# Local attention on Trainium2: the keys' copy on VectorE and the queries' copy between the exponentials, in the steps without an output projection

## Chip, core and metric

The kernel runs on one core of a Trainium2 chip. The metric is the device time of one execution in microseconds (us). Five engines with queues of their own work in parallel: TensorE (PE in the profile; its weight loads are PEld), VectorE (DVE), ScalarE (ACT), GpSimd (POOL) and SyncE (SP, which issues the DMAs).

## What is computed

The input is x with 8 batches of 512 rows and 256 columns, all in float32. Four residual blocks follow each other:

```
x = x + attention_a(layernorm(x))
x = x + layers(layernorm(x))
x = x + attention_b(layernorm(x))
x = x + layers(layernorm(x))
```

`layers` applies two layers, each a local attention and a feedforward part. The change lies in the local attention:

```
h = shift_token(x)
q, k, v = split(h @ wqkv)            # 8 heads of 64
q = l2norm(q) * qs ; k = l2norm(k) * ks
q, k = rotary_xpos(q, k)
# windows of 128 rows; a row sees its own window and the one before,
# masked to i - 128 <= j <= i
o = softmax(q k^T * 8, masked) v
x = x + o @ wo
```

The feedforward part is a layer norm, a product, a gate with GELU and a second product, added to x.

## The kernel before

**Stages.** The batches are worked in two groups of four. For each group the stages are: full attention (`attention_a`); then twice local attention (`attention_f`) and feedforward; then the second full attention (`attention_b`); then again twice local attention and feedforward. So there are eight stages of local attention. The profile names their tiles f0x, f0y, f1x and f1y (group, and first or second block); both layers of a block share a name.

**Tiles and steps.** A stage of local attention has 4 batches with 4 tiles of 128 rows each, 16 tiles in all (`nt`). One step of the loop in `run`, written out in `a_step`, works on three tiles at a time. For tile `step` it makes scores, softmax and values; this comes in two units of four heads each, `even` and `odd`. For tile `step + 1` it turns the rotated queries and keys so that the head dimension lies on the partitions (`turn_tile`, then `keep_tile`). For tile `step + 2` it makes the projections to queries, keys and values, the rotation and the norms. Steps -5 to -1 are handed out one by one to the stage before, which runs them among its own last steps. Steps 0 to 16 are the stage's own.

**One unit.** PE makes the scores (`scores`, L616). VectorE adds the mask and takes the maxima (`maxima`, four times L638), then L649 multiplies them by the inverse norm, with both inputs in SBUF. ScalarE makes four exponentials (`exponentials`, recorded at L241 of the helper `function`). In `divided`, VectorE takes the reciprocal of the sums (L719) and ScalarE divides (L735). PE turns the probabilities (`turn`, L681), VectorE copies them from PSUM (`keep_turned`, L692), and PE multiplies them with the values (`values`, L706).

**Around it.** `queries_and_keys` is the product at L510 (tile pqk). VectorE rotates it (`rotate`, L538 and L541), POOL adds both parts (`rotated`, twice L552), ScalarE squares (`squared`, L562), VectorE sums the squares (`norms`, L569), and POOL makes the inverse root (L266 and L267, of the helper `inv_sqrt`). The next step multiplies the keys by it on VectorE (`normalize_keys`, L583). `turn_tile` (L592) makes eight 128x128 turns into one PSUM tile of two banks, queries in one and keys in the other; `keep_tile` copies them to SBUF, both on ScalarE (L601 and L602). The scores of the next step read both copies. `keep_values` (L740), `project` (L748) and `add` (L755) are the output projection of a tile that is done.

**Order.** In steps 0 to 16 every instruction is chained to the one issued before it on its engine (`kept_order`), so each engine's queue is the order of the calls in `a_step`. The feedforward stage that follows lends pieces to steps 5 and 11 to 14 (`ahead()`), which are chained in the same way: in step 11 row statistics (L276 and L277), in step 12 the normalized rows hn (eight times L283), in step 13 one turn and its copy (L295 and L911). What the following stage issues after that is not chained on POOL. One such instruction is L923, which adds a bias to the rows y on POOL, 128x1024 elements, and which the builder has placed behind the inverse root of step 12. In the first layer, step 0 also normalizes the rows of a later batch (four times L283). POOL's adds at L552 wait by hand for the newest L649 (the list `marks`).

**Which steps project.** `project_next` makes one output projection a step. Steps 12 and 13 defer theirs to the last steps (`deferring`), and in step 0 none is due yet. Steps 14 to 16 have no new tile to project (`projecting` is false) and another order.

## Time and profile before

| what | us |
|---|---|
| median of 3 runs | 4423.52 (4421.06 to 4423.76) |
| the profiled execution | 4422.09 |
| its span in the trace | 4420.3 |
| busy: PE, DVE, ACT, POOL | 4195.3, 3100.1, 2699.3, 1175.5 |
| granted TensorE clock, mean | 0.993 of full speed |

The profile is one execution. A line of the timeline gives start, duration, engine, line of the code, operation, output and inputs, and how many neighbours were merged (x8). A bracket at its end tells how long the engine had stood idle before it and what ended that. [...] A line such as L241 can be that of a helper.

| line, engine | what | shape | us each |
|---|---|---|---|
| L601, ACT | copy of the turned queries | 128x512 from PSUM | 0.56 |
| L602, ACT | copy of the turned keys | 128x512 from PSUM | 0.58 |
| L740, DVE | copy of the values' product | 128x512 from PSUM | 0.68 |
| L569, DVE | sums of squares | 128x16 from 128x1024 | 1.21 |
| L267, POOL | power of -0.5 | 128x16 | 2.93 |
| L241, ACT | one exponential | 128x256 | 0.59 |

### The profile page before, as it was taken

To read this page: it belongs to the slowest core of one execution; us is meant where nothing else is said; L and a number is where in the kernel's file an instruction comes from. 1 tells how busy PE (TensorE), PEld (TensorE's weight loads), DVE (VectorE), ACT (ScalarE), POOL (GpSimd) and SP (SyncE) were. 2 spreads that over 40 slices of the span, in tenths; PEclk is the share of its full clock that TensorE was granted. 3 is DMA by queue.
4 is the path that set the end of the run, shared out by engine and by line. 5 is a ranking of instruction groups with operands and counts; after the bars stand their busy time and mean duration, and the time that the engine had idled before them with its cause. 6 is when DMAs were issued, how large, how long until landed. Compare 5 with 4: busy or idle time off the path is not lost.

```text
span 4420.3 us, 70595 instructions
## 1 busy us (share of the span) xinstructions
PE 4195.3 (95%) x26580; PEld 2536.5 (57%) x26580; DVE 3100.1 (70%) x7497; ACT 2699.3 (61%) x6316; POOL 1175.5 (27%) x1220
## 2 busy tenths in 40 slices
PE   9999999999888899999999999999999888999999
PEld 5666556655555465566566665565545554655655
DVE  6678737747999786377466786377479997863773
ACT  6777517716898675176167675276178996742761
POOL 0014214312222342143200242243122223422431
PEclk9999999999999999999999999999999999999999
DMA  2000000000000000000100000000000000000000
GB/s 82 1 22 4 23 3 23 3 24 20 2 1 1 20 4 7 4 22 13 53 30 1 20 3 24 22 4 23 5 21 1 2 1 20 4 6 23 3 4 23
DMA packets 51092, 63.36 MB, mean 14 GB/s; under 512 B 6336, under 2 KB 45504, under 8 KB 50752
## 3 DMA queue, kind: packets, MB, share of 16 engines
q1 hardware_dynamic: 50752, 58.85, 4.1%
q8 instruction: 211, 3.46, 0.3%
q14 instruction: 129, 1.06, 0.1%
HBM read 46.28 MB, written 4.19 MB: 11 GB/s over the span
## 4 chain that ended last, share of the span: by engine, by line
PE 74%; DVE 14%; ACT 9%; issue 1%; POOL 1%; DMA 0%; SPq 0%; POOLq 0%; ACTq 0%; DVEq 0%
PE pu_g1x L932 3%; PE pu_g0x L932 3%; PE pu_g0y L932 3%; PE pu_g1y L932 3%; PE s_a L389 3%; PE o_a L425 3%; PE ppt_a L414 3%; PE pqk_f1x L510 2%; PE pqk_f1y L510 2%; PE pqk_f0y L510 2%; PE pqk_f0x L510 2%; DVE pt_b L1274 2%; PE ppt_b L1269 2%; DVE r_b L1220 2%; PE pu_b L1085 1%; DVE num_b L1239 1%
## 5 line engine op out<-in xcount | busy, mean ns | idle before, releaser
L1269 PE MATMUL ppt_b<-ident,num_b 128*128 128x128 f32 x1280 | 227.5, 294 | 93.1 <-DVE pt_b L1274 63.3
L1269 PEld LDWEIGHTS ppt_b<-ident,num_b 128*128 128x128 f32 x1280 | 139.7, 144 | 279.3 <-ACT num_b L241 92.6
L241 ACT ACTIVATE num_b<-num_b,most_b 128x512 f32<-128x512 f32 (+3 forms) x512 | 280.6, 553 | 21.4 <-POOL most_b L1249 21.2
L1232 POOL TENSOR_TENSOR num_b<-num_b,causal 128x256 f32<-128x256 f32 x256 | 200.8, 797 | 258.9 <-ACT num_b L1226 258.9
L1274 DVE COPY pt_b<-ppt_b 128x512 f32<-128x512 f32 (+1 forms) x352 | 224.4, 637 | 36.8 <-PE ppt_b L1269 35.3
L1239 DVE CUSTOM_DVE_ANT_0 num_b<-num_b,r_b 128x512 f32<-128x512 f32 (+3 forms) x512 | 238.1, 512 | 3.7 <-POOL num_b L1232 3.7
L241 ACT ACTIVATE p_a<-s_a,nm_a 128x512 f32<-128x512 f32 x256 | 173.7, 683 | 105.0 <-DVE nm_a L393 101.9
L1216 DVE TENSOR_TENSOR t_b<-den_b,r_b 128x1024 f32<-128x1024 f32 (+1 forms) x176 | 197.3, 1121 | 25.9 <-ACT r_b L241 25.6
L1197 PE MATMUL den_b<-st_b,st_b 18*128 18x384 f32 (+3 forms) x1024 | 207.0, 476 | 7.5 <-ACT yT_b L1075 4.1
L1220 DVE SCALAR_TENSOR_TENSOR r_b<-t_b,r_b 128x1024 f32<-128x1024 f32 (+1 forms) x176 | 208.6, 1185 | 0.2
L393 DVE TENSOR_REDUCE nm_a<-s_a 128x2 f32<-128x1024 f32 x128 | 156.4, 1223 | 70.4 <-PE s_a L389 70.4
L241 ACT ACTIVATE r_b<-den_b 128x1024 f32<-128x1024 f32 (+1 forms) x176 | 165.8, 942 | 52.5 <-PE den_b L1197 30.1
L241 ACT ACTIVATE p_f0y<-p_f0y,nm_f0y,rn_f0y 128x256 f32<-128x256 f32 (+1 forms) x256 | 143.8, 563 | 80.6 <-DVE nm_f0y L649 80.5
L241 ACT ACTIVATE p_f1y<-p_f1y,nm_f1y,rn_f1y 128x256 f32<-128x256 f32 (+1 forms) x256 | 143.8, 563 | 80.6 <-DVE nm_f1y L649 80.5
L1197 PE MATMUL dot_b<-st_b,st_b 16*128 16x384 f32 (+3 forms) x1024 | 191.6, 475 | 0.0
L241 ACT ACTIVATE p_f1x<-p_f1x,nm_f1x,rn_f1x 128x256 f32<-128x256 f32 (+1 forms) x256 | 143.8, 564 | 76.0 <-DVE nm_f1x L649 75.9
L241 ACT ACTIVATE p_f0x<-p_f0x,nm_f0x,rn_f0x 128x256 f32<-128x256 f32 (+1 forms) x256 | 143.8, 564 | 75.3 <-DVE nm_f0x L649 75.2
L407 ACT ACTIVATE p_a<-p_a,sums_a 128x512 f32<-128x512 f32 x256 | 171.9, 719 | 26.5 <-DVE sums_a L405 26.5
L552 POOL TENSOR_TENSOR ro_f1x<-ro_f1x,rs_f1x 128x512 f32<-128x512 f32 x64 | 80.2, 1276 | 360.8 <-DVE rs_f1x L541 144.8
L552 POOL TENSOR_TENSOR ro_f0x<-ro_f0x,rs_f0x 128x512 f32<-128x512 f32 x64 | 80.2, 1275 | 360.6 <-DVE rs_f0x L541 144.8
L241 ACT ACTIVATE r_b<-r_b 128x1024 f32<-128x1024 f32 (+1 forms) x176 | 172.5, 980 | 5.7
L1226 ACT ACTIVATE num_b<-dot_b 128x1024 f32<-128x1024 f32 (+1 forms) x176 | 164.8, 937 | 3.1 <-PE dot_b L1197 3.1
(356 smaller groups left out, 11238.9 us busy)
## 6 DMA issues: line engine op xcount, KB each, us to landing
x<-in_x SPq DMA_DIRECT2D x8, 512.0 KB
out<-x SPq DMA_DIRECT2D x8, 512.0 KB
wf_0x<-in_f_wqkv SPq DMA_DIRECT2D x2, 1536.0 KB
wf_0y<-in_f_wqkv SPq DMA_DIRECT2D x2, 1536.0 KB
wf_1x<-in_f_wqkv SPq DMA_DIRECT2D x2, 1536.0 KB
wf_1y<-in_f_wqkv SPq DMA_DIRECT2D x2, 1536.0 KB
wg_0x<-in_f_w SPq DMA_DIRECT2D x2, 1386.0 KB
wg_0y<-in_f_w SPq DMA_DIRECT2D x2, 1386.0 KB
```

Of the source, the lines that this page charges most:

```text
L241: i = nc.scalar.activation(out, in_, func, **more).ins
L407: nc.scalar.activation(p[:, odd], p[:, odd], AF.Identity, scale=some[:, odd : odd + 1])
L510: nc.tensor.matmul(dst.rearrange("p h d -> p (h d)"), lhsT=hTs[b][:, k, t * P : (t + 1) * P], rhs=wqkv[:, k, c * INNER : (c + 1) * INNER], ...
L932: nc.tensor.matmul(pu[: cols.stop - cols.start, c], lhsT=w1[:, k, cols], rhs=hT[:, k, :], start=(k == 0), stop=(k == 1),)
L1197: return nc.tensor.matmul(s[:, a, m * width : (m + 1) * width], lhsT=left[at, j, past:width], rhs=right[at, j, :width], start=True, stop=True,
L1216: nc.vector.tensor_mul(t[:, :, :cols], den[:, :, :cols], r[:, :, :cols])
L1220: nc.vector.scalar_tensor_tensor(r[:, :, :cols], t[:, :, :cols], 2.0, r[:, :, :cols], ALU.subtract, ALU.mult)
L1226: nc.scalar.activation(num[:, :, :cols], dot[:, :, :cols], AF.Square, scale=-0.5)
L1232: nc.gpsimd.tensor_add(own, own, causal.unsqueeze(1).to_broadcast([P, 2, P]))
L1239: nc.vector.tensor_tensor_reduce(out=s4[:, a, m, :], in0=s4[:, a, m, :], in1=r4[:, a, m, :], scale=-1.0, scalar=LOWEST, op0=ALU.mult, op1= ...
L1269: nc.tensor.transpose(ppt[:, k, :], p[:, a, k * P : (k + 1) * P], ident)
L1274: nc.vector.tensor_copy(pt[:, a, :nblocks, :], ppt[:, :nblocks, :])
```

## The change

In steps 0, 12 and 13 of each stage (`light`) the order of the calls after the values' projection becomes: two of the four exponentials of the odd unit; `keep_values`; the turn of the even unit and its copy; the turn of the next tile; the queries' copy on ScalarE and the keys' copy on VectorE; the other two exponentials; the norms. Before, the order was: four exponentials, `keep_values`, the turn of the even unit and its copy, the norms, the turn of the next tile, and both copies on ScalarE. What comes after (`divided`, `values` and so on) is as it was. The other steps keep their order, and the work done is the same.

```diff
-        def keep_tile(at):
+        def keep_tile(at, by_vector=False):
...
             nc.scalar.copy(qT, pqt[:, 0])
-            nc.scalar.copy(kTs[b][:, :, t * P : (t + 1) * P], pqt[:, 1])
+            copy = nc.vector.tensor_copy if by_vector else nc.scalar.copy
+            copy(kTs[b][:, :, t * P : (t + 1) * P], pqt[:, 1])
...
-        def exponentials(unit):
+        def exponentials(unit, halves=(0, 1)):
...
-            p, nm, rn = ps[unit], nms.pop(unit), rns[at]
+            p, nm, rn = ps[unit], nms[unit], rns[at]
...
-            for odd in range(2):
+            for odd in halves:
...
             deferring = step in (nt - 4, nt - 3)
+
+            light = step == 0 or deferring
...
-            if projecting:
+            if projecting and light:
+                exponentials(odd, (0,))
+                on(keep_values, step - 1)
+                on(turn, even, nu)
+                on(keep_turned, even, nu)
+                on(turn_tile, step + 1)
+                keep_tile(step + 1, True)
+                exponentials(odd, (1,))
+                on(norms, step + 2)
+            elif projecting:
                 on(exponentials, odd, nu)
                 on(keep_values, step - 1)
                 on(turn, even, nu)
...
                     on(turn_tile, step + 1)
                     on(keep_tile, step + 1)
+            if projecting:
                 if not deferring:
                     project_next()
```

## The prediction

> **What bounds the kernel now.** I read the page's busy shares and its chain of work first, then the list of waits, then the timeline of one local-attention stage, of which the program has eight (two layers in each of four blocks).

> ```profile
> PE 4195.3 (95%) x26580; PEld 2536.5 (57%) x26580; DVE 3100.1 (70%) x7497; ACT 2699.3 (61%) x6316; POOL 1175.5 (27%) x1220
> PE 74%; DVE 14%; ACT 9%; issue 1%; POOL 1%; DMA 0%; SPq 0%; POOLq 0%; ACTq 0%; DVEq 0%
> ```

> TensorE (PE) carries three quarters of the chain; VectorE (DVE) and ScalarE (ACT) carry it only where PE stands idle. The change touches steps 0, 12 and 13 of each stage, 24 steps in all. Sixteen of them end in a PE wait for the keys' copy, eight of 1.59 us after step 0 and eight of 1.59 to 1.65 after step 12: 25.8 us, 0.58% of the span. That is the largest prize. The first stage:

> ```profile
> 316.16 0.57 ACT L601 COPY qT_f0x<-pqt_f0x 128x512 f32<-128x512 f32 x1
> 316.47 0.44 POOL L266 TENSOR_SCALAR rn_f0x<-ss_f0x 128x16 f32<-128x16 f32 x1
> 316.63 0.59 ACT L602 COPY kT_f0x<-pqt_f0x 128x512 f32<-128x512 f32 x1
> 317.11 1.29 ACT L735 ACTIVATE p_f0x<-p_f0x,sums_f0x 128x128 f32<-128x128 f32 x4
> 317.27 1.13 PE L616 MATMUL s_f0x<-kT_f0x,qT_f0x 64*128 64x256 f32 x8 [1.59 <-ACT kT_f0x L602]
> 318.33 0.66 PE L681 MATMUL ppt_f0x<-ident,p_f0x 128*128 128x128 f32 x4
> 318.83 3.60 PE L510 MATMUL pqk_f0x<-wf_0x,hT_f0x 128*128 128x512 f32 x8
> ...
> 479.11 0.69 DVE L692 COPY pt_f0x<-ppt_f0x 128x512 f32<-128x512 f32 x1
> 479.72 1.21 DVE L569 TENSOR_REDUCE ss_f0x<-sq_f0x 128x16 f32<-128x1024 f32 x1
> 481.21 0.18 DVE L719 RECIPROCAL sums_f0x<-sums_f0x 128x4 f32<-128x4 f32 x1 [0.28 <-ACT p_f0x L241]
> 481.27 0.27 POOL L266 TENSOR_SCALAR rn_f0x<-ss_f0x 128x16 f32<-128x16 f32 x1
> 481.63 3.03 POOL L267 TENSOR_TENSOR rn_f0x<-rn_f0x,neg_half 128x16 f32<-128x16 f32 x1
> 484.63 2.34 POOL L923 TENSOR_TENSOR y_0x<-y_0x,b 128x1024 f32<-128x1024 f32 x1
> 484.86 2.12 DVE L649 SCALAR_TENSOR_TENSOR nm_f0x<-nm_f0x,rn_f0x 128x4 f32<-128x4 f32 x1
> 486.91 0.68 DVE L583 TENSOR_TENSOR ro_f0x<-ro_f0x,rn_f0x 128x512 f32<-128x512 f32 x1
> 488.24 0.66 PE L706 MATMUL o_f0x<-pt_f0x,v_f0x 128*64 128x128 f32 x8 [0.91 <-DVE pt_f0x L692]
> ...
> 496.39 0.17 DVE L719 RECIPROCAL sums_f0x<-sums_f0x 128x4 f32<-128x4 f32 x1
> 496.47 0.57 ACT L602 COPY kT_f0x<-pqt_f0x 128x512 f32<-128x512 f32 x1
> 496.95 1.71 ACT L735 ACTIVATE p_f0x<-p_f0x,sums_f0x 128x256 f32<-128x256 f32 x4
> 497.51 1.64 PE L681 MATMUL ppt_f0x<-ident,p_f0x 128*128 128x128 f32 x8 [0.43 <-ACT p_f0x L735]
> ```

> Columns: start and duration in us, engine, line. Three things are to be seen. In step 0 the turns of the probabilities (L681) follow the scores closely, and they need the divisions (L735), which end at 318.40. After step 12 a 128x4 operation on VectorE takes 2.12 us: it stands until GpSimd's (POOL's) L923 ends at 486.97. Elsewhere the same line takes 0.16 to 0.17; all eight that start inside an L923 take 1.92 to 2.15. In step 13 VectorE's reciprocal (L719) follows the reduction L569 without a gap.

> **The parts and their prices.** ScalarE loses a copy that holds it 0.47 us (316.16 to 316.63 for its twin). VectorE gains one of 128x512 from PSUM: 0.68 to 0.69 in L692 and L740, with the next instruction 0.61 after its start. Both copies now stand ahead of the last two exponentials and wait for PE's turn of the tile; behind the one on VectorE are queued L569, the reciprocal and all later VectorE work; behind L569, POOL's two steps of the inverse root (L266, L267). No DMA is issued or moved, and SP's queue is not passed. The scores now wait for two engines; a semaphore instruction of PE's queue at L616 takes 0.05 us, so 0 to 0.05, hidden because the turns behind the scores wait for ACT anyway.

> Step 0. The tile's turn ends on PE at 315.08. Queries: 315.21 to 315.78. Keys: about 315.12 to 315.80. The scores can start at 315.85, 1.42 earlier, and end at 316.98. But L569 slides from 314.31 to 315.73, ends 316.94, and the reciprocal comes at 316.86 instead of 316.30. The divisions start 0.21 to 0.25 after a reciprocal where nothing else holds them (489.56 and 489.77), so at 317.1, where they were: what ACT gains by the lost copy, the late reciprocal takes. The fourth turn follows the fourth division at about 318.44, and the next projection (pqk) starts 0.13 later, at 318.57 instead of 318.83: **0.26 us won**. From there PE is nearly gapless to step 12, so the gain stays. POOL's root ends about 0.4 later (320.3), L583 waits until then; the copy behind it ends at 321.65, before PE wants it at 322.1: hidden.

> Step 12. Tile turned at 479.95 (478.91 and 1.04); keys on VectorE from 479.99, L569 at 480.60, ending at E = 481.81 instead of 480.93. L266 had been held by POOL's own add L552 to 481.18; now it follows E by 0.09 (so it does at 496.47, 496.56): 481.90, which is 0.63 later, and L267 and L923 with it. L923 starts 0.09 + 0.36 + 2.89 (the undisturbed stage) = 3.34 after E. The reciprocal starts 0.08 before E and L649 always 3.65 behind it (481.21 to 484.86; 837.56 to 841.21): E + 3.57. So L649 again finds L923 running and stands until it ends, 0.63 later than now; L583, the copy of the turned probabilities and PE's values (a wait of 0.91 now) go with it. The earlier scores are thus worth nothing here: **0.63 us lost** in seven stages. In the second stage L569 moves from 835.95 to 837.00 and L266 from 837.51 to 838.30: 0.79.

> Step 13. The tile's turn ends at 494.37, VectorE is free at 495.26; keys 495.26, L569 495.87 to 497.08, reciprocal 497.00, divisions 497.23 instead of 496.95. The turns and scores behind them, and the whole tail of the stage, wait on this: **0.28 us lost**. ACT's 0.47 was free to be won, but the late reciprocal takes it and more.

> Sum: 7 x (0.63 + 0.28 - 0.26) + (0.79 + 0.28 - 0.26) = 5.4 us. The profiled execution took 4422.09 (span 4420.3 and 1.8 around it), which makes 4427.5; the median of the runs shown, 4423.5, lies 1.4 higher, so 4428.9 against it, plus 0.12%. A measurement of this kernel can tell about 0.2%, 8.8 us, from no change; this is inside.

> [...]

> **Rivals.** (1) L649 gets in ahead of L923. L266 took 0.44 instead of 0.27 where it started 0.08 behind a VectorE row operation (316.47 above), as it now would in step 12, and L267 took 3.03 instead of 2.92 once: L923's lead of 0.23 could become -0.05. Then L649 takes 0.16 and the exponentials start 1.4 sooner; L583 still stands behind L923 (to about 487.75), the copy ends at 489.0, the reciprocal of step 13 comes 0.66 sooner, the keys' copy of step 13 takes 0.34 of that back, and the divisions start at 496.63: 0.32 won over both steps. With step 0, 0.58 a stage: -4.6 us, 4418.9. For it: the lead is within the scatter; against: POOL leads in most combinations, and L1220 is held up (1.71 instead of 1.22) where it starts 0.10 after a GpSimd operation.

> (2) Slower by over 0.2%: VectorE's copy is itself held by the rope add L552, beside which it runs in all three steps. Held to L552's end it would start 1.29, 1.2 and 1.03 us later (316.39, 481.18, 496.27), and some 1.2 + 1.84 + 1.31 us a stage would be lost: 35 us, 4458. It decides from 0.15 us held per copy (1.10 a stage). Against it: L692's copies that start beside L552 take 0.69 and 1.23, those that don't 0.68 and 1.22.

> (3) The wait goes, and PE keeps it: 25.8 us, 4398. Against it stand the divisions in step 0 and L923 in step 12.

> (4) Nothing: the edits cancel, within 2 us.

> **How the numbers follow.** Forecast 0.48, rival 1 0.30, rival 2 0.08, rival 3 0.08, rival 4 0.06. Bounds of the forecast: copy's hold 0.61 to 0.69, L266's delay 0 to 0.17, each passed on in steps 12 and 13: 0.5 to 1.0 a stage, 4427 to 4432. Rival 1 reaches down to 4416. The range 4416 to 4432 leaves out rivals 2 and 3, 0.16. Faster by over 0.2% is rival 3, 0.08; slower, rival 2, 0.08; within, the rest, 0.84.

> **What would show it.** Right: the 1.6 us waits of the scores gone after steps 0 and 12, pqk only 0.26 sooner; L569 1.4, 0.9 and 0.6 later; L923 0.6 later with L649 still about 2 us; divisions of step 13 0.28 later. Wrong: L649 of 0.16 after step 12 (rival 1); a keys' copy on VectorE over 0.8 us (rival 2); L923 elsewhere in POOL's queue, since it is not in the hand-written order and the build places it anew.

## The result and the profile after

| | before | changed |
|---|---|---|
| median, us | 4422.04 (5 runs, 4421.06 to 4423.76) | 4440.52 (5 runs, 4436.02 to 4442.29) |
| ratio | | 1.004 (95% interval 1.0029 to 1.005) |
| profiled execution: span, granted TensorE clock | 4420.3, 0.993 | 4438.7, 0.991 |

The changed kernel is 0.4% slower: 18.5 us where the forecast had 5.4, and above the range given (4416 to 4432). In the changed kernel the keys' copy is L603, and the lines behind it have moved: scores L617, maxima L639, L649 is now L650, the turns L682, their copy L693, values L707, reciprocal L720, divisions L736, and the bias add L923 is L936. The page's busy row and its chain:

```profile
PE 4212.5 (95%) x26580; PEld 2540.6 (57%) x26580; DVE 3116.4 (70%) x7521; ACT 2691.5 (61%) x6292; POOL 1177.7 (27%) x1220
PE 75%; DVE 14%; ACT 8%; issue 1%; POOL 1%; DMA 0%; SPq 0%; POOLq 0%; ACTq 0%; DVEq 0%
```

VectorE has 24 instructions more and ScalarE 24 fewer, as the change says. But PE, with the same 26580 matmuls, is busy for 17.2 us longer (4195.3 before). About half of this is no slower work: after steps 0 and 12 the four turns L682 now follow the divisions one by one, and their row counts 1.21 where it was 0.66 (some 9 us in all). The other half is in the products pqk and pv (together 9 us), which have become slower in places; no step of the prediction allowed for that.

Step 0 of the first stage, from the timeline of the changed kernel (start, duration, engine, line; the bracket is the idle time before it and what ended it; rows of one engine can overlap: L569 starts at 317.71, 0.08 before the 0.69 of L603 are over). The trace of the changed kernel runs 1.28 us behind that of before already at the start of this step, so a time of before is to be raised by 1.28 for a comparison.

```profile
316.49 0.58 ACT L601 COPY qT_f0x<-pqt_f0x 128x512 f32<-128x512 f32 x1
317.10 0.69 DVE L603 COPY kT_f0x<-pqt_f0x 128x512 f32<-128x512 f32 x1 [1.42 <-ACT qT_f0x L601]
317.71 1.21 DVE L569 TENSOR_REDUCE ss_f0x<-sq_f0x 128x16 f32<-128x1024 f32 x1
317.85 1.13 PE L617 MATMUL s_f0x<-kT_f0x,qT_f0x 64*128 64x256 f32 x8 [0.89 <-DVE kT_f0x L603]
318.83 0.17 DVE L720 RECIPROCAL sums_f0x<-sums_f0x 128x4 f32<-128x4 f32 x1
319.04 1.28 ACT L736 ACTIVATE p_f0x<-p_f0x,sums_f0x 128x128 f32<-128x128 f32 x4 [1.01 <-DVE sums_f0x L720]
319.49 1.21 PE L682 MATMUL ppt_f0x<-ident,p_f0x 128*128 128x128 f32 x4 [0.51 <-ACT p_f0x L736]
320.54 3.60 PE L510 MATMUL pqk_f0x<-wf_0x,hT_f0x 128*128 128x512 f32 x8
```

To be seen: the keys' copy on VectorE does not start with PE's turn, which ended at 316.37, but 0.03 after the end of the queries' copy on ScalarE. VectorE stands idle for 1.42 us ahead of it, and the sums of squares (L569) and the reciprocal (L720) stand behind it. The projection pqk comes 0.43 later than before (318.83 + 1.28 = 320.11), not 0.26 sooner.

Steps 12 and 13 of the same stage:

```profile
481.66 0.57 ACT L601 COPY qT_f0x<-pqt_f0x 128x512 f32<-128x512 f32 x1
482.26 0.69 DVE L603 COPY kT_f0x<-pqt_f0x 128x512 f32<-128x512 f32 x1 [0.92 <-ACT qT_f0x L601]
482.87 1.21 DVE L569 TENSOR_REDUCE ss_f0x<-sq_f0x 128x16 f32<-128x1024 f32 x1
...
484.00 0.17 DVE L720 RECIPROCAL sums_f0x<-sums_f0x 128x4 f32<-128x4 f32 x1
...
484.24 0.29 POOL L266 TENSOR_SCALAR rn_f0x<-ss_f0x 128x16 f32<-128x16 f32 x1 [1.50 <-DVE sums_f0x L720]
...
484.62 3.08 POOL L267 TENSOR_TENSOR rn_f0x<-rn_f0x,neg_half 128x16 f32<-128x16 f32 x1
...
487.60 0.16 DVE L650 SCALAR_TENSOR_TENSOR nm_f0x<-nm_f0x,rn_f0x 128x4 f32<-128x4 f32 x1
487.67 2.35 POOL L936 TENSOR_TENSOR y_0x<-y_0x,b 128x1024 f32<-128x1024 f32 x1
487.73 2.83 DVE L583 TENSOR_TENSOR ro_f0x<-ro_f0x,rn_f0x 128x512 f32<-128x512 f32 x1
...
490.49 0.68 DVE L693 COPY pt_f0x<-ppt_f0x 128x512 f32<-128x512 f32 x1
...
491.22 0.66 PE L707 MATMUL o_f0x<-pt_f0x,v_f0x 128*64 128x128 f32 x8 [1.92 <-DVE pt_f0x L693]
...
497.25 0.69 DVE L603 COPY kT_f0x<-pqt_f0x 128x512 f32<-128x512 f32 x1 [0.27 <-ACT qT_f0x L601]
```

The same wait stands in step 12 (idle 0.92) and step 13 (0.27). In 23 of the 24 steps the bracket of L603 names the queries' copy. And the meeting with the bias add went the other way: L650 gets in 0.07 ahead of L936 and takes 0.16, and L583, the next operation of VectorE, stands in its place until L936 ends (2.83 instead of 0.68). PE then waits 1.92 for the copied turns behind L583.

The third thing shows in the windows view of the changed kernel (columns: the stretch, its length, then busy us and count of PE, PEld, DVE, ACT and POOL, then the granted TensorE clock PEclk, DMA share and GB/s):

```profile
673.59:677.00 3.41, 2.01 (x19) 1.24 (x17) 2.50 (x6) 2.40 (x9) 1.96 (x4) 1.00 0.02 5
677.44:680.85 3.41, 3.41 (x7) 1.74 (x7) 1.68 (x7) 2.70 (x9) 2.30 (x1) 0.50 0.00 0
4271.24:4274.65 3.41, 1.50 (x14) 0.81 (x14) 3.41 (x4) 2.44 (x9) 1.34 (x2) 1.00 0.07 19
4275.09:4278.50 3.41, 3.41 (x8) 1.40 (x5) 3.03 (x12) 1.35 (x2) 0.80 (x1) 0.50 0.07 21
```

In the second and fourth row PE works for the whole 3.41 us, at half clock. The same product pqk that takes 3.60 elsewhere takes 5.02 there:

```profile
675.22 1.13 PE L617 MATMUL s_f0x<-kT_f0x,qT_f0x 64*128 64x256 f32 x8 [0.89 <-DVE kT_f0x L603]
676.87 1.36 PE L682 MATMUL ppt_f0x<-ident,p_f0x 128*128 128x128 f32 x4 [0.51 <-ACT p_f0x L736]
678.02 5.02 PE L510 MATMUL pqk_f0x<-wf_0x,hT_f0x 128*128 128x512 f32 x8
```

The profile of before has no such half-clock stretch in its eight stages of local attention; this one has seven. The next table splits the 18.4 us between the two spans: by how much PE's start of the same instruction moved against the profile of before, for each stage, from the product pv of step 0 to the first product of the feedforward.

| stage | step 0 | steps 12 and 13 | whole stage | what stands out |
|---|---|---|---|---|
| 1 | +0.43 | +0.69 | +0.98 | |
| 2 | +1.95 | +2.32 | +4.29 | half clock from 677.4 and 851.5; L650 stands for 2.26 |
| 3 | +0.43 | +1.74 | +2.42 | L650 stands for 2.26 |
| 4 | +2.13 | +0.68 | +2.80 | half clock from 1896.0 |
| 5 | +0.43 | +0.69 | +1.11 | half clock from 2691.3; PE's wait behind it shrinks to 0.37 |
| 6 | +0.43 | +0.68 | +1.10 | |
| 7 | +0.42 | +2.27 | +2.71 | half clock from 3913.3 |
| 8 | +1.99 | +2.34 | +4.34 | half clock from 4101.0 and 4275.1 |

Stages 1, 5 and 6 lose 1.0 to 1.1 us with nothing else to see in the time, which makes some 8.5 in eight. The two in which L650 stands lose about 1.1 more each, 2.2. What is left of the 19.75, some 9 us, falls on the half-clock stretches (1.5 to 1.7 us for one in step 0: 1.95, 2.13 and 1.99 against 0.43). The rest of the span adds 1.3 ahead of the first stage and takes 2.6 back between the stages.

### The profile page after: what moved, and what is told of

It reads as the page before. It is cut to its first block, busy times and chain, and to the rows that moved or that the text cites. A ratio compares the mean times of both kernels' runs of the same rounds, so it can differ in the third digit from the quotient of the medians.

```text
span 4438.7 us, 70599 instructions
## 1 busy us (share of the span) xinstructions
PE 4212.5 (95%) x26580; PEld 2540.6 (57%) x26580; DVE 3116.4 (70%) x7521; ACT 2691.5 (61%) x6292; POOL 1177.7 (27%) x1220
## 3 DMA queue, kind: packets, MB, share of 16 engines
q14 instruction: 129, 1.06, 0.1%
## 4 chain that ended last, share of the span: by engine, by line
PE 75%; DVE 14%; ACT 8%; issue 1%; POOL 1%; DMA 0%; SPq 0%; POOLq 0%; ACTq 0%; DVEq 0%
PE pu_g0x L945 3%; PE pu_g1x L945 3%; PE pu_g0y L945 3%; PE pu_g1y L945 3%; PE s_a L389 3%; PE o_a L425 3%; PE ppt_a L414 3%; PE pqk_f0x L510 2%; PE pqk_f1x L510 2%; PE pqk_f0y L510 2%; PE pqk_f1y L510 2%; PE ppt_b L1282 2%; DVE pt_b L1287 2%; DVE r_b L1233 2%; PE pu_b L1098 1%; DVE num_b L1252 1%
## 5 line engine op out<-in xcount | busy, mean ns | idle before, releaser
L241 ACT ACTIVATE num_b<-num_b,most_b 128x512 f32<-128x512 f32 (+3 forms) x512 | 280.6, 554 | 19.8 <-POOL most_b L1262 19.6
L241 ACT ACTIVATE p_a<-s_a,nm_a 128x512 f32<-128x512 f32 x256 | 173.7, 683 | 105.4 <-DVE nm_a L393 102.3
L241 ACT ACTIVATE r_b<-den_b 128x1024 f32<-128x1024 f32 (+1 forms) x176 | 165.8, 942 | 53.9 <-PE den_b L1210 31.4
L241 ACT ACTIVATE p_f0y<-p_f0y,nm_f0y,rn_f0y 128x256 f32<-128x256 f32 (+1 forms) x256 | 143.9, 564 | 78.8 <-DVE nm_f0y L650 78.8
L241 ACT ACTIVATE p_f1y<-p_f1y,nm_f1y,rn_f1y 128x256 f32<-128x256 f32 (+1 forms) x256 | 143.9, 564 | 76.5 <-DVE nm_f1y L650 76.4
L241 ACT ACTIVATE p_f0x<-p_f0x,nm_f0x,rn_f0x 128x256 f32<-128x256 f32 (+1 forms) x256 | 143.9, 564 | 73.4 <-DVE nm_f0x L650 73.3
L241 ACT ACTIVATE p_f1x<-p_f1x,nm_f1x,rn_f1x 128x256 f32<-128x256 f32 (+1 forms) x256 | 143.9, 564 | 71.5 <-DVE nm_f1x L650 71.5
L241 ACT ACTIVATE r_b<-r_b 128x1024 f32<-128x1024 f32 (+1 forms) x176 | 172.5, 980 | 5.6
L552 POOL TENSOR_TENSOR ro_f0x<-ro_f0x,rs_f0x 128x512 f32<-128x512 f32 x64 | 80.3, 1277 | 358.7 <-DVE nm_f0x L650 145.6
L552 POOL TENSOR_TENSOR ro_f1x<-ro_f1x,rs_f1x 128x512 f32<-128x512 f32 x64 | 80.3, 1275 | 355.7 <-DVE rs_f1x L541 144.8
```

The lines of the kernel that those rows point to most:

```text
L241: i = nc.scalar.activation(out, in_, func, **more).ins
```

## The experiments

The theory after this reading had three parts. The keys' copy waits for the queries' copy, since both read one PSUM tile, and what it delays is the work queued behind it on VectorE, the sums of squares above all. Whether L650 or L583 meets the bias add decides steps 12 and 13. And TensorE's waits call its half clock (theory D in the expectations). The rivals: that VectorE's copy itself is what costs, or the scores behind it; that the bias add alone is the cause in steps 12 and 13; and that the half clock is a state of the single execution. Medians are compared with runs of the kernel before on the same chip (4421.5 to 4422.9).

**Keys in a tile of their own.** The turned keys go to a PSUM tile of their own (pkt, 128x512), so that no other engine reads the tile that VectorE copies.

```diff
+            halves = [pqt[:, 0], pqt[:, 1]]
+            if own_bank:
+                halves[1] = ps_mm.tile([P, 4, P], F32, tag="mm", name=f"pkt_{n}")
...
-                on(turn_tile, step + 1)
+                turn_tile(step + 1, True)
```

> The changed kernel, but in steps 0, 12 and 13 the turned keys go into a PSUM tile of their own (the one-bank tile that the values' projection uses), so that the keys' copy on VectorE no longer waits for the queries' copy on ScalarE. Theory A (the copy's wait for the other reader is the step that was missed): the keys' copy starts within 0.1 us of the end of the turn or of VectorE's own queue, some 0.7 us sooner in steps 0 and 12; in stages without a half-clock window the loss falls from 1.1 us to about 0.6; with that alone some 4436, and less if smaller gaps on TensorE also bring fewer half-clock windows (down to 4427). Rival B (the later sums of squares on VectorE are the loss, whoever the copy waits for): the stages stay at 1.1 us and the time at 4440. Theory C (the half-clock windows of TensorE's clock are chance and no part of the change): their number stays at about 17 in the profile.

Measured: 4424.73 (11 runs), ratio 1.0005 (0.9996 to 1.0014). The timeline of step 0 (the tile pkt holds the keys; lines are shifted by 3):

```profile
314.52 0.60 PE L595 MATMUL pkt_f0x<-ident,ro_f0x 128*128 128x128 f32 x4
...
315.16 0.69 DVE L606 COPY kT_f0x<-pkt_f0x 128x512 f32<-128x512 f32 x1 [0.73 <-PE pkt_f0x L595]
315.77 1.21 DVE L569 TENSOR_REDUCE ss_f0x<-sq_f0x 128x16 f32<-128x1024 f32 x1
316.00 1.13 PE L620 MATMUL s_f0x<-kT_f0x,qT_f0x 64*128 64x256 f32 x8 [0.29 <-DVE kT_f0x L606]
316.89 0.17 DVE L723 RECIPROCAL sums_f0x<-sums_f0x 128x4 f32<-128x4 f32 x1
```

The copy now starts 0.04 after PE, and step 0 wins 0.27 in all eight stages, where the prediction had 0.26. So the copy as such is as cheap as forecast, and the wait for the other reader is the difference. In steps 12 and 13 the operation behind the maxima gets in ahead of the bias add in seven stages; the three of them without a half-clock stretch come to -0.64 to -0.69 for the whole stage (rival 1 had -0.58). In the one stage where it stands (from 2055.98 for 2.26) the whole comes to +0.56; the forecast had +0.65 for that case. Four stages had half-clock stretches and came to +0.78 to +1.21, so that the eight together lose 2.6 us in this profile; in the median, too, the kernel isn't faster than before.

**Only step 0.** `light` holds in step 0 alone.

```diff
-            light = step == 0 or deferring
+            light = step == 0
```

> The changed kernel with the new order in step 0 alone; steps 12 and 13 are as before. From the profile's stages (0.43 us lost by the first projection after step 0, and half-clock windows after step 0 in three stages of eight, 1.6 us each): 4422 plus 3.4 plus 5, some 4430. If the loss lies in steps 12 and 13 alone: 4422 to 4424. By the prediction's own sum for step 0 (0.26 us won a stage): 4420.

Measured: 4426.47 (11 runs), ratio 1.001 (1.0001 to 1.0019). Step 0 loses 0.42 in all eight stages, the whole stage 0.27 to 0.56, all eight 3.4 us, near what the median says (3.8). There is no half-clock stretch in its stages. So step 0 is a plain loss of 0.42, and the larger part of the 18.5 us comes from steps 12 and 13 and from the half clock, which step 0 alone did not call here.

**The sums of squares ahead of the copy.** In the changed kernel `norms` is called ahead of `turn_tile`; the keys' copy still waits for ScalarE's.

```diff
                 on(keep_turned, even, nu)
+                on(norms, step + 2)
                 on(turn_tile, step + 1)
                 keep_tile(step + 1, True)
                 exponentials(odd, (1,))
-                on(norms, step + 2)
```

> The changed kernel with one call moved back: in steps 0, 12 and 13 the sums of squares stand on VectorE ahead of the keys' copy again, as in the kernel before. The copy still waits for ScalarE's copy of the queries. If the damage is done by what is queued on VectorE behind the waiting copy (sums of squares, POOL's inverse root, its bias add): POOL's root and bias add start where they did before, 1.4 us sooner against the tile's turn; the stages fall from 1.1 us lost to about 0 (0.4 won in step 0, 0 in step 12, 0.3 lost in step 13): 4418 to 4428 with the windows that remain. If the damage is the copy's wait as such, through the scores: no change, 4440.

Measured: 4423.05 (11 runs), ratio 1.0000 (0.9991 to 1.0009): 17 us faster than the changed kernel by moving one line. From its timeline, step 0:

```profile
313.41 1.21 DVE L569 TENSOR_REDUCE ss_f0x<-sq_f0x 128x16 f32<-128x1024 f32 x1
...
314.91 0.69 DVE L603 COPY kT_f0x<-pqt_f0x 128x512 f32<-128x512 f32 x1 [0.29 <-ACT qT_f0x L601]
...
315.65 1.14 PE L617 MATMUL s_f0x<-kT_f0x,qT_f0x 64*128 64x256 f32 x8 [0.89 <-DVE kT_f0x L603]
315.87 0.18 DVE L720 RECIPROCAL sums_f0x<-sums_f0x 128x4 f32<-128x4 f32 x1 [0.27 <-ACT p_f0x L241]
```

The copy still stands behind the queries' copy and the scores still wait for it by 0.89, exactly as in the changed kernel. But the reciprocal waits for ScalarE again and not for the reduction. Step 0 wins 0.34, steps 12 and 13 come to -0.10 and +0.24, the stage to -0.2, and no half-clock stretch falls in the stages. That settles the first part: what cost was not the copy, nor the scores, but what was queued behind the copy on VectorE.

**The bias add late, without the change.** The kernel before, with the bias add of the feedforward's first tile made to wait for the maxima of step 14.

```diff
+                    if step == nt - 2:
+                        phase["port"] = marks[-1]
...
+            if b == batches[0]:
+                tc.add_manual_dep(i, phase["port"].name, WAIT, reason="port")
```

> The kernel before, with POOL's bias add of the following stage made to wait for the last maxima of step 14, so that it no longer runs beside the small VectorE operation of step 13. Nothing else changes. Theory E (the two exclude each other, and that wait of 2 us is on the path that sets the end): that operation takes 0.16 us in all eight stages, TensorE's wait for the values of step 13 (0.9 us) goes, and the stage gains 0.9 to 1.9 us: 4407 to 4415. Rival F (TensorE or ScalarE takes the place of the wait): the operation is short, the time stays at 4422.

Measured: 4406.85 (5 runs), ratio 0.9966 (0.9953 to 0.9978); every stage wins 1.96 to 2.01 but the second, which wins 1.78; about half of it is in step 12 and half in step 13. The timeline of step 12:

```profile
481.43 3.02 POOL L267 TENSOR_TENSOR rn_f0x<-rn_f0x,neg_half 128x16 f32<-128x16 f32 x1
...
484.66 0.16 DVE L649 SCALAR_TENSOR_TENSOR nm_f0x<-nm_f0x,rn_f0x 128x4 f32<-128x4 f32 x1
484.74 0.68 DVE L583 TENSOR_TENSOR ro_f0x<-ro_f0x,rn_f0x 128x512 f32<-128x512 f32 x1
```

With no add beside them L649 takes 0.16 and L583 0.68. The stand behind the bias add was worth 2 us a stage in the kernel before already.

**The bias add late, in the changed kernel.** The same edit on the changed kernel, of which this is the part that makes the add wait:

```diff
+            if b == batches[0]:
+                tc.add_manual_dep(i, phase["port"].name, WAIT, reason="port")
```

> Changed kernel, with the tensor add of the feedforward's first tile (L936) made to wait for the maxima of step 14, so that neither L650 nor L583 can stand behind it. It tells apart what in steps 12 and 13 is the add's lock and what is the late sums of squares. If the lock were all of it: step 0 keeps +0.42, steps 12 and 13 come to -0.98 and -0.99 as in the kernel before with the same edit: -1.55 in each stage, about 4410. If the late sums of squares and their reciprocal cost of themselves: step 0 +0.42, steps 12 and 13 together -1.25 (as with the keys in a tile of their own) or worse, down to -0.5: -0.8 to -0.1 in each stage, 4415 to 4422, a few us more if half-clock windows fall in the stages.

Measured: 4423.78 (11 runs), ratio 1.0003 (0.9994 to 1.0012). Step 0 +0.42 to +0.43, step 12 about -0.57, step 13 +0.21: about +0.05 in most stages without half clock, against -1.99 for the same edit without the change. So the change costs 2.0 us a stage also when nothing stands behind the add: 0.42 in step 0, 0.41 in step 12, 1.20 in step 13. The rival that the add is all of it would have given 4410; it falls. Step 13 with the add late, without the change (the first two rows) and with it:

```profile
491.96 1.21 DVE L692 COPY pt_f0x<-ppt_f0x 128x1024 f32<-128x1024 f32 x1
494.78 1.71 ACT L735 ACTIVATE p_f0x<-p_f0x,sums_f0x 128x256 f32<-128x256 f32 x4
...
493.81 1.22 DVE L693 COPY pt_f0x<-ppt_f0x 128x1024 f32<-128x1024 f32 x1
495.11 0.69 DVE L603 COPY kT_f0x<-pqt_f0x 128x512 f32<-128x512 f32 x1
497.04 1.71 ACT L736 ACTIVATE p_f0x<-p_f0x,sums_f0x 128x256 f32<-128x256 f32 x4 [0.79 <-DVE sums_f0x L720]
```

PE is 1.06 behind at the step's product pv (489.78 against 488.72). The divisions come 2.26 later, so 1.20 beyond that.

**The bias add late, with the keys in a tile of their own.** Both edits together:

```diff
+                turn_tile(step + 1, True)
...
+                tc.add_manual_dep(i, phase["port"].name, WAIT, reason="port")
```

> The changed kernel with the turned keys in a PSUM tile of their own and POOL's bias add made to wait for the maxima of step 14. It tells what the new order of steps 12 and 13 is worth without the bias add. If the add was all that spoiled step 12: below 4406.9, the kernel before with the add moved. If the late sums of squares cost there as well, through POOL's inverse root and the reciprocal: 0.3 to 0.8 us a stage more than that kernel in steps 12 and 13, 0.27 less in step 0: 4407 to 4412, more where half-clock windows fall.

Measured: 4409.87 (6 runs), ratio 0.9973 (0.9961 to 0.9984); -1.5 a stage, of it 0.27 in step 0. It is 0.5 a stage worse than the bias add late alone: step 12 wins 0.3 more, but step 13, which won 1.0 there, wins nothing. The sums of squares still come later by the copy's own time without the wait for the other reader; that this is what steps 12 and 13 pay for was not tried by itself.

**Idle products in PE's waits.** To test whether PE's waits call the half clock, products that nobody uses were put into them, in three versions of the changed kernel. The first had long ones (all of 512 columns):

```diff
+                if step - 1 in (0, nt - 4):
+                    filled(step, 1, "b")
...
+            if light:
+                filled(step, 2, "a")
```

> The changed kernel with idle products on TensorE where it now waits: two of 512 columns behind the values in steps 0, 12 and 13, and one ahead of the next step's first turns after steps 0 and 12. They write a PSUM tile that nobody reads. Theory D (TensorE's idle time in these steps halves its clock for windows of 3.4 us, seven more than before, about 1.6 us each): those windows go from steps 0, 12 and 13, and the time falls by about 10 us to some 4430, though TensorE has more to do. Rival C (the windows are chance): they stay, and the time is 4440 or more, since the idle products can only add.

Measured: 4447.64 (5 runs, 4438.17 to 4450.83), ratio 1.0055 (1.0043 to 1.0068), the rival's time (4440 or more). The products delayed the stages by themselves (2.1 us each, 3.2 the first). In its profile, which is of the fastest of the five executions, no stage of local attention has a half-clock stretch, and the mean clock of the five was 0.992 to 0.994. The second had shorter ones (one of 256 columns, one of 512):

```diff
+                if step - 1 in (0, nt - 4):
+                    filled(step, 256, "b")
...
+            if light:
+                filled(step, 512, "a")
```

> The changed kernel with smaller idle products than the ones tried before: one of 512 columns behind the values of steps 0, 12 and 13 (about 0.5 us), one of 256 ahead of the next step's first turns after steps 0 and 12 (0.25 us). Both fit into TensorE's present waits, so they should cost nothing: 1.1 us a stage as in the changed kernel where no half-clock window falls. If idle time of TensorE calls the windows: fewer of them in the local attention, 4428 to 4436, and a higher mean clock than 0.991. If not: 4440 and 0.991.

Measured: 4437.54 (5 runs), ratio 1.0032 (1.0019 to 1.0044), neither one theory's number nor the other's. Its profile left the waits of 1.8 to 1.9 us ahead of the values in step 13 open, and one half-clock stretch fell in the stages. The third closed these too (against the second):

```diff
                 if step - 1 in (0, nt - 4):
                     filled(step, 256, "b")
...
+                if step == nt - 3:
+                    filled(step, 512, "c")
+                    filled(step, 256, "d")
...
-            if light:
+            if light and step < nt - 3:
                 filled(step, 512, "a")
```

> Changed kernel, with idle products (no use is made of what they compute) in TensorE's queue at its own waits: 512 columns ahead of the scores after the keys' copy in steps 0 and 12, 256 columns ahead of the turns in steps 1 and 13, and 512 and 256 columns in step 13 ahead of the products with the values (a wait of 1.92 us in the profile of the changed kernel, left open in the last such run). Theory D (TensorE's empty time in one cell of the 3.41 us grid calls the half-clock windows): the direct shift of about 1.1 us in each of eight stages stays, about 9 us, and the windows of the stages go: 4429 to 4434, at most one or two windows in the eight stages, granted clock 0.993 or 0.994 in most executions. Rival (the windows have another cause, for instance the run's own state): 4436 to 4442 as with the changed kernel, clock 0.991 or 0.992.

Measured: 4438.14 (5 runs, 4437.77 to 4442.49), ratio 1.004 (1.0028 to 1.0053). In its profile no stage of local attention has a half-clock stretch, and its executions had a mean clock of 0.992 to 0.994, those of the changed kernel 0.990 to 0.991 and those of the kernel before 0.992 to 0.995. So the clock is what theory D has, and the half clock isn't a state of the single execution. But the time is the rival's (4436 to 4442). L650 now stood behind the bias add in five stages instead of two (2.00 to 2.40 lost in each, 1.08 to 1.18 in the three others), which cost some 3 us more. The stages' sum fell from 19.75 to 14.2 us; outside the stages the span lost 0.8 us more ahead of the first and took back little between them (0.3 instead of 2.6). The test supports the cause of the half clock and doesn't give its price.

**The best of it.** Only step 0, sums of squares ahead of the copy, keys in a tile of their own, bias add late.

```diff
-            light = step == 0 or deferring
+            light = step == 0
...
+                on(norms, step + 2)
+                turn_tile(step + 1, True)
...
+                tc.add_manual_dep(i, phase["port"].name, WAIT, reason="port")
```

> A version put together from what has been seen: the new order in step 0 alone, with the sums of squares ahead of the keys' copy and the turned keys in a PSUM tile of their own; steps 12 and 13 as in the kernel before; POOL's bias add made to wait for the maxima of step 14. Against the kernel before with only the bias add moved (4406.9): step 0 should win 0.3 to 0.45 us a stage, 2.4 to 3.6 in all: 4403 to 4405. If step 0 wins nothing once its scores come early: 4407.

Measured: 4402.62 (5 runs, 4400.88 to 4403.02), ratio 0.9954 (0.9941 to 0.9968), the fastest of all kernels here: -0.34 in step 0 and -0.99 in each of steps 12 and 13. Against its own runs of before it wins 18.9 us, the bias add late alone 15.8; the 3.1 between them is about what step 0 gives, 8 x 0.34 = 2.7.

## Why the prediction was wrong

**The step that failed** is the first one of each part: "The tile's turn ends on PE at 315.08. Queries: 315.21 to 315.78. Keys: about 315.12 to 315.80." The prediction let both copies wait for PE alone. In the built program the keys' copy waits for ScalarE's queries' copy, the other reader of the PSUM tile (its bracket names that copy in 23 of the 24 steps), and it starts about 0.7, 0.7 and 0.3 later than written in steps 0, 12 and 13 (in step 0 at 317.10 - 1.28 = 315.82 against 315.12; in step 13 against the moment at which VectorE is free). The prediction asked of the added instruction only what it reads and what queues behind it, not what else reads the same tile.

**Step 0.** "0.26 us won" became 0.43 lost; the difference is 0.69, the wait. The reasoning behind it held: the reciprocal follows the reduction, the divisions follow the reciprocal by 0.21 (318.83 to 319.04), pqk follows them. With the wait taken away the step gave -0.27.

**Step 12.** "E + 3.34" for the bias add against "E + 3.57" for L649 was not what came: E is 484.08, L936 came at E + 3.59 and L650 at E + 3.52. POOL's L266 followed E by 0.16 and not 0.09, L267 began at E + 0.54 where the forecast has E + 0.45, and it took 3.08 and not 2.92. Rival 1 had named a late root as what could turn the meeting (a longer L266, which took 0.29 and so did not come, and a longer L267), and its case happened in six of eight stages. (The 3.03 that the prediction gives for L267 as a single case stands in three of the eight stages of before.) In all 32 such meetings in the four changed profiles read for it (the changed kernel, keys in a tile of their own, the second and third filling) L267 took either 2.92, and then the operation behind the maxima started 0.10 after the add and stood for 2.26 to 2.27, or 3.07 to 3.08, and then it started 0.06 ahead and took 0.16. The second stage of the changed kernel shows the first case:

```profile
843.51 2.92 POOL L267 TENSOR_TENSOR rn_f0x<-rn_f0x,neg_half 128x16 f32<-128x16 f32 x1
...
846.40 2.35 POOL L936 TENSOR_TENSOR y_0x<-y_0x,b 128x1024 f32<-128x1024 f32 x1
846.51 2.26 DVE L650 SCALAR_TENSOR_TENSOR nm_f0x<-nm_f0x,rn_f0x 128x4 f32<-128x4 f32 x1
```

In both cases the operation behind the maxima starts 2.98 to 2.99 after L267 does, and what L267 takes more, 0.155, is as long as that operation. Of the 128 runs of L267 in the changed kernel's profile only the six of these meetings take over 2.93. So the longer L267 may be an effect of the other's getting in first as well as its cause; which it is, and what decides so close a meeting, isn't shown by any row. The price that the forecast set on its own case was near: +0.56 measured with the wait taken away, +0.65 forecast; rival 1's was -0.58, measured -0.64 to -0.69.

**Step 13.** "0.28 us lost" by the late reciprocal: with nothing behind the add, step 13 kept 1.20 of loss against the same edit without the change. The wait in this step is the small part of it: with the keys in a tile of their own 1.02 were left. In the rows above VectorE's copy of the turned probabilities already comes 0.79 late (493.81 against 491.96, less the 1.06 that PE is behind): that is step 12's lateness, which PE feels only here. The wait adds 0.17 and the keys' copy 0.60 ahead of the sums of squares, 1.56 in all. Of this 0.36 is won back: the divisions follow the reciprocal by 0.20 (496.84 to 497.04) and not by 0.56 (494.22 to 494.78), since ScalarE has one copy less.

**The half clock** was in no term of the sum, and no rival had it. It is some 9 of the 19.75 us that the stages lose in the profiled execution. All seven stretches begin whole multiples of 3.413 us apart (851.5 - 677.4 = 51 times, 4275.1 - 677.4 = 1054 times): a grid that stands through the execution and lies at another place in the profile of before, 1.15 us away counted from the start of the span. The share of PE's busy time in the cell of 3.41 us that ends 0.4 us ahead of a stretch was 0.44 to 0.59 in these seven (2.01 and 1.50 of 3.41 in the rows above). Over the twelve profiles of this study, before and changed among them, the cells sort like this, those that are in part at half clock left out (the lag of 0.4 us is chosen because it sorts well, so it is fitted):

| PE's busy share in the cell | cells | followed by half clock |
|---|---|---|
| under 0.35 | 40 | 39 |
| 0.35 to 0.60 | 284 | 89 |
| 0.60 to 0.85 | 1488 | 18 |
| 0.85 and more | 13309 | 0 |

So four of the seven stretches follow a cell that holds the waits of 0.89 to 0.94 and 0.51 in step 0, three a cell with the 1.8 to 1.9 ahead of the values in step 13, and where the grid lies decides which cells are that empty. A share of 0.44 isn't enough by itself:

```profile
489.29:492.70 3.41, 1.49 (x17) 1.10 (x16) 3.41 (x5) 2.43 (x8) 0.86 (x2) 1.00 0.07 21
493.14:496.55 3.41, 3.41 (x20) 2.21 (x19) 3.33 (x12) 2.69 (x6) 1.28 (x2) 1.00 0.07 21
```

Here, in the changed kernel's first stage, a cell as empty as that at 4271 left the clock at 1.00. The kernel before had 17 cells of 0.35 to 0.60 in its stages, and no stretch followed; the changed one had 19, and seven did. With the new order in step 0 alone there were 14 and no stretch. That the waits call the half clock is thus supported, by the table, by the clock of all five executions and by the first and third filling, but it isn't shown to be all: what exactly is counted stays open, why the cells of before were harmless too, and so does the change's price in clock for an average execution.

**What was right.** VectorE's copy takes 0.69 in all 24 steps, in 22 of them beside POOL's L552, so rival 2 fell; rival 3 fell, the waits of 1.59 became 0.89 and 0.94 and the divisions kept the end; the tail after step 13 moved with the divisions. The chance of 0.08 for slower by over 0.2% was set on rival 2 alone; the loss came from the forecast's own path.

## What to carry to other kernels

When two instructions on different engines are made to share one PSUM tile, look in the trace for an order between them: here the copies of the tile's two halves ran one after the other (in step 0 the keys' copy started 0.03 after the end of the queries'), and with a tile for each the keys' copy started 0.04 after PE's turn. Price what is queued behind the later one, not only what reads its result. Ahead of a moved instruction, put what others wait for: the same copy behind the sums of squares cost nothing that the medians tell (4423.05, ratio 1.0000). And where TensorE is 95% busy, as here, read the clock in every stage that was touched: this change left waits of 0.51, 0.89 and 1.92 us in the steps it touched, and beside some 11 us of their own the stages lost some 9 us on half-clock stretches in this profile.

## What the runs showed of the hardware that was not expected

In the changed kernel the 128x4 VectorE operation with both inputs in SBUF that meets the 128x1024 bias add on POOL either starts 0.06 ahead of it and takes 0.16, or starts 0.10 behind it and takes 2.26. In the six stages in which the small one (L650) escapes, the next one (L583) starts 0.06 after the add and takes 2.83: getting ahead moved the stand to the next operation and did not remove it.
